# Graph network with layer norm: silu of the last three node groups made by ScalarE alone

## The chip, the cores and the metric

The kernel runs on one core of a Trainium2 chip. The metric is the device time of one execution in microseconds (us); smaller is better. A profile is one further execution, recorded instruction by instruction. In it PE is TensorE, DVE is VectorE, ACT is ScalarE, POOL is GpSimd and SP is the engine that issues most transfers.

## The reference

There are 12,500 nodes with 128 features and 400,000 edges sorted by destination. Each edge carries a message; the messages are summed by destination; each node's sum goes through two small products with silu between them; the result is added to twice the node's own value and normalized.

```python
rbf = jnp.exp(-(distances[:, None] - centers) ** 2 / (2.0 * width * width))
cut = 0.5 * (jnp.cos(jnp.pi * distances / CUTOFF) + 1.0) * (distances <= CUTOFF)
W = (jax.nn.silu(rbf @ fw1 + fb1) @ fw2 + fb2) * cut[:, None]
messages = (h[src] @ pw + pb) * W
agg = jax.ops.segment_sum(messages, dst, num_segments=num_atoms)
h_new = h + (jax.nn.silu(agg @ mw1 + mb1) @ mw2 + mb2)
x = layernorm(x + h_new)        # here h is x
```

The change concerns only the line with `mw1` and `mw2`, and there only how silu is made for the last nodes.

## The kernel before, in words

The order of instructions is written out by hand: every engine executes its own list in the order in which the program issues it, and an instruction waits until what it needs is there.

The work has four stages. First, `project` multiplies all nodes by `pw` and stores the result in memory. Beside it, `pack` drops the edges beyond the cutoff and lays the rest out in 141 steps (`NQ`) of 512 edges. Then the loop over the steps q follows: GpSimd gathers 512 projected source rows with four indirect transfers (L643); TensorE and ScalarE make the edge's filter W (L693, L699, L707, L710); VectorE multiplies filter and gathered rows to messages (`message`, L717) and builds a selection matrix (`place`, L726); TensorE sums the messages by destination (`sum_up`, L742); VectorE adds these sums into `aggT`, the sums of all nodes held on the chip with features as rows (`add`, L765), one or two steps later.

The nodes are finished in 25 groups of four row tiles, 512 nodes each, named by their first row tile t0 = 0, 4, ..., 96; group 96 has 212 nodes. The steps of finishing a group are:

- `node_first` (L772): a bank of PSUM takes the bias and the product with `mw1` (L776, L777). ScalarE writes t = tanh(z/2) to a tile `zt` (L779). The bank is kept.
- `node_silu` (L782): VectorE makes zs = (t + 1) * z from `zt` and the bank (L786). That is twice silu(z). The bank is free then.
- `node_second` (L790): another bank takes bias (L274) and zs times `late["mw2"]` (L277), which is `mw2` halved, so that the factor two goes out again. `rows_times` (L271) issues these products.
- `node_stats` (L795): VectorE adds twice x (L801) and takes the statistics of each row (L805).
- `scales` (L807): for up to four groups together, 18 short VectorE operations on at most 16 columns make the reciprocal root and the shift.
- `normalize` (L836): ScalarE (L844), and at the very end VectorE too (L841), scale the rows; SP issues the store (L137).

As edges are sorted by destination, early nodes are complete before the loop ends. A table `begin` (L888 to L896) says at which step each group starts its four stages, beginning at step 70. Groups whose four stages all come before step 141 are called `early`. Group 88 starts at step 139 but can't end inside the loop: it alone is `last`. It gets `node_first` at step 139 and `node_silu` at step 140, both inside the loop, in `nodes(q)` (L900), which is issued ahead of the step's message. Groups 92 and 96 are in no table. They, and the second half of group 88, are issued by `finish` (L860) behind the loop.

`finish` issues: `node_first` of 92 and 96; then for 88, 92 and 96 in turn `node_second`, `node_stats`, and, after the statistics of one group, `node_silu` of the next group; then `scales` of the three and the normalizations.

There are four banks handed out by `bank()` in the order in which they were given back. Tiles named `zt` share a tag of three buffers with `xT`, tiles named `zs` a tag of three with `hp`.

A branch (L1099) repeats the whole sum in a general way if the layout of the edges broke an assumption; with these inputs it isn't taken. It calls `finish` a second time with all groups.

Of the kernel before, what the change touches and what calls it, by code (L numbers as in the profile page):

```python
# [10 lines left out]
F32 = mybir.dt.float32  # L11
BF16 = mybir.dt.bfloat16
I32 = mybir.dt.int32
AF = mybir.ActivationFunctionType
# [5 lines left out]
P = 128  # L20
# [6 lines left out]
QE = QT * P  # L27
# [30 lines left out]
def kernel(  # L58
# [37 lines left out]
    nc = tc.nc  # L96
# [16 lines left out]
    work = ctx.enter_context(tc.tile_pool(name="work", bufs=2))  # L113
# [4 lines left out]
    def load_x(t0, name="x4", bufs=8):  # L118
        t = work.tile([P, 4, H], F32, name=name, bufs=bufs)
        node_dma(t0, t, x, False)  # L120
        x_sb[t0] = t

    def rows(t0, n=4):
        return [min(P, N - t * P) for t in range(t0, min(t0 + n, NT))]

    def alike(r):


        full = sum(1 for m in r if m == P)
        return [v for v in ((0, full, P), (full, len(r) - full, r[-1])) if v[1]]  # L130
# [65 lines left out]
    for t0 in range(0, 4 * AHEAD_X, 4):  # L196
# [3 lines left out]
    fw2_sb, mw1_sb, mw2_sb = (keep.tile([H, H], F32, name=k)  # L200
                              for k in ("fw2_sb", "mw1_sb", "mw2_sb"))
# [16 lines left out]
    bias_b = {}  # L218
# [52 lines left out]
    def rows_times(to, lT, w, bias_b, r):  # L271

        for a, c, m in alike(r):
            nc.tensor.matmul(to[:m, a:a + c, :], ones_b[:, :m], bias_b[:, :c, :], start=True,  # L274
                             stop=False)
            for k in range(a, a + c):
                nc.tensor.matmul(to[:m, k, :], lT[:, k * P:k * P + m], w, start=False,  # L277
                                 stop=(k == a + c - 1))
# [25 lines left out]
    free = [ps.tile([P, 512], F32, name=f"bank{k}", bufs=1) for k in range(4)]  # L304
    held = []

    def bank():

        while not free:
            go_on(held[0])  # L310
        return free.pop(0)
# [455 lines left out]
    late = {}  # L767


    z_of, zs_of, py_of, st_of = {}, {}, {}, {}  # L770

    def node_first(t0):  # L772

        n = sum(rows(t0))
        pz = bank()
        nc.tensor.matmul(pz[:, :n], bias_b["mb1"][:, 0, :], ones_b[:, :n], start=True, stop=False)  # L776
        nc.tensor.matmul(pz[:, :n], mw1_sb, aggT[:, t0 * P:t0 * P + n], start=False, stop=True)  # L777
        t = work.tile([P, QE], F32, name="zt", tag="xT", bufs=3)
        nc.scalar.activation(t[:, :n], pz[:, :n], AF.Tanh, scale=0.5)  # L779
        z_of[t0] = pz, t  # L780

    def node_silu(t0):  # L782
        n = sum(rows(t0))
        pz, t = z_of.pop(t0)
        s = work.tile([P, QE], F32, name="zs", tag="hp", bufs=3)
        nc.vector.scalar_tensor_tensor(s[:, :n], t[:, :n], 1.0, pz[:, :n], op0=OP.add, op1=OP.mult)  # L786
        free.append(pz)
        zs_of[t0] = s

    def node_second(t0):  # L790

        py_of[t0] = bank()
        rows_times(py_of[t0].rearrange("p (k f) -> p k f", k=4), zs_of.pop(t0), late["mw2"], bias_b["mb2"], rows(t0))

    def node_stats(t0, st):  # L795

        r = rows(t0)
        y, b = x_sb[t0], py_of.pop(t0)
        py = b.rearrange("p (k f) -> p k f", k=4)
        for a, c, m in alike(r):  # L800
            nc.vector.scalar_tensor_tensor(y[:m, a:a + c], y[:m, a:a + c], 2.0, py[:m, a:a + c],  # L801
                                           op0=OP.mult, op1=OP.add)
        free.append(b)
        for k, m in enumerate(r):
            nc.vector.bn_stats(st[:m, k, :], y[:m, k, :])  # L805
# [30 lines left out]
    def normalize(t0, rs, by, both=False):  # L836

        y = x_sb.pop(t0)
        for k, m in enumerate(rows(t0)):
            if both and k:  # L840
                nc.vector.tensor_scalar(y[:m, k, :], y[:m, k, :], rs[:m, k:k + 1], by[:m, k:k + 1],  # L841
                                        op0=OP.mult, op1=OP.add)
            else:
                nc.scalar.activation(y[:m, k, :], y[:m, k, :], AF.Identity, bias=by[:m, k:k + 1],  # L844
                                     scale=rs[:m, k:k + 1])
        node_dma(t0, y, out, True)
# [3 lines left out]
    def scaled(group, st):  # L850

        rs, by = scales(st, sum(len(rows(t)) for t in group))
        ready.extend((t, rs[:, t - group[0]:], by[:, t - group[0]:]) for t in group)

    def statistics():
        st = work.tile([P, 16, 6], F32, name="st")
        nc.vector.memset(st, 0.0)
        return st

    def finish(these, have=()):  # L860

        every = list(have) + these
        for t0 in every[:4]:
            if t0 not in x_sb:
                load_x(t0)
        for k, t0 in enumerate(every):
            if k + 4 < len(every) and every[k + 4] not in x_sb:
                load_x(every[k + 4])
            if k % 4 == 0:
                st = statistics()  # L870
            for t1 in every[len(have) if k == 0 else k + 2:k + 3]:
                if t1 not in have:
                    node_first(t1)
            if k == 0 and not have:
                node_silu(t0)
            node_second(t0)
            node_stats(t0, st[:, k % 4 * 4:])
            if k + 1 < len(every):
                node_silu(every[k + 1])
            if k % 4 == 3 or k + 1 == len(every):  # L880
                scaled(every[k // 4 * 4:k + 1], st)
            if ready and k + 1 < len(every):
                normalize(*ready.pop(0))
        while ready:
            normalize(*ready.pop(0), both=True)
# [10 lines left out]
        at_q += 3 if at_q < NQ - 12 else 2  # L896
    last = [t0 for t0 in begin if begin[t0][3] >= NQ]
    early = [t0 for t0 in begin if t0 not in last]

    def nodes(q):  # L900

        if ready:
            normalize(*ready.pop(0))
        for k, t0 in enumerate(early + last):
            if begin[t0][0] - 5 == q:
                load_x(t0)
            if begin[t0][3] == q and t0 in early:
                if k % 4 == 0:
                    st_of[0] = statistics()
                node_stats(t0, st_of[0][:, k % 4 * 4:])  # L910
                if k % 4 == 3 or k + 1 == len(early):
                    scaled(early[k // 4 * 4:k + 1], st_of[0])
            if begin[t0][2] == q and t0 in early:
                node_second(t0)
            if begin[t0][0] == q:
                node_first(t0)
            if begin[t0][1] == q:
                node_silu(t0)
        if q == NQ - 4:
            for t0 in range(0, NT, 4):  # L920
                if t0 not in begin:
                    load_x(t0)
# [170 lines left out]
    for q in range(added(NQ), NQ):  # L1093
        base_of(q)
        add(q)
    finish([t0 for t0 in tiles if t0 not in begin], last)


    with tc.If(total > 0):  # L1099
# [51 lines left out]
        if E % QE:  # L1151
            again(E - QE, QT - E % QE // P)
        finish(tiles)


# [24 lines left out]
```

## Time and profile before

| what | us |
|---|---|
| median of 3 runs | 816.37 |
| lowest, highest | 815.54, 817.31 |
| time of the profiled execution | 819.14 |
| its span, first to last instruction | 817.3 |
| TensorE busy in the span | 604.2 (74%) |
| VectorE busy | 587.5 (72%) |
| ScalarE busy | 381.1 (47%) |
| GpSimd busy | 569.8 (70%) |
| mean granted clock of TensorE | 0.851 of full |
| L786 on VectorE, 128x512 | 0.67 to 0.68 each |
| L786 on VectorE, 128x212 | 0.36 |
| last gather issued | 784.57 (from the span's start) |
| last addition into `aggT` ends | 792.7 |
| last normalization ends | 810.9 |

The page's busy shares are means over stages of different kind, so they say little about one stage. A row of a chain view gives the start, the length and the instruction (engine, output tile, line) of one link; "issue" is time in which the engine waited for nothing that the profile shows, and a name such as DVEq is the queue of an engine, which loads registers or issues. A row of a group gives busy time, mean duration in ns, and then the idle time of the engine just before such instructions with what ended it. The granted clock is what share of its full clock TensorE was given.

### The profile page before, as it was taken

What the parts mean: (1) busy time and instruction counts of PE and PEld (TensorE: products, weight loads), DVE (VectorE), ACT (ScalarE), POOL (GpSimd) and SP (SyncE); (2) the same over time, 40 slices, a digit from 0 to 9 for tenths busy, and PEclk for the clock granted to TensorE, in tenths of its full rate; (3) what the DMA queues carried; (4) which work ended last, traced back from release to release, by engine and by line L of the source; (5) the groups of instructions that cost most, each with busy time, mean ns of one, the idle gap of its engine ahead of it and who ended that gap; (6) DMA issues with size and microseconds to landing.
All of it is one profiled execution on the core that took longest, in us unless ns stands there. A gap on an engine that the chain in (4) does not pass through costs nothing.

```text
span 817.3 us, 11550 instructions
## 1 busy us (share of the span) xinstructions
PE 604.2 (74%) x3492; PEld 475.7 (58%) x3492; DVE 587.5 (72%) x1785; ACT 381.1 (47%) x536; POOL 569.8 (70%) x585
## 2 busy tenths in 40 slices
PE   6777878768776777866588678887777887688661
PEld 5766657547664555655456556665555665566551
DVE  7962568989978877979796677657566565756764
ACT  6536656434644353253354254636444633454421
POOL 1375477777777777777777777777777777777730
PEclk9978899977987776778779788999889989889875
DMA  6968734342234223332531622723622642371221
GB/s 198 263 201 246 191 85 105 90 117 75 74 107 112 65 65 112 103 78 53 144 87 52 164 65 79 194 68 104 170 79 58 159 122 78 80 188 52 81 83 48
DMA packets 88189, 91.86 MB, mean 112 GB/s; under 512 B 13864, under 2 KB 67832, under 8 KB 88120
## 3 DMA queue, kind: packets, MB, share of 16 engines
q1 hardware_dynamic: 69320, 52.77, 22.6%
q0 software_dynamic: 18544, 38.17, 18.6%
q8 instruction: 29, 0.48, 0.2%
q14 instruction: 40, 0.33, 0.1%
q10 hardware_dynamic: 256, 0.11, 0.1%
HBM read 75.29 MB, written 15.71 MB: 111 GB/s over the span
## 4 chain that ended last, share of the span: by engine, by line
DVE 24%; POOL 20%; DMA 20%; issue 16%; PE 14%; ACT 3%; DVEq 2%; SPq 0%; POOLq 0%; ACTq 0%
POOL quad L643 20%; DMA quad<-proj,srci 18%; DVE hot L726 4%; PE sums L742 4%; PE bank L277 3%; DVE aggT L765 3%; DVE quad L726 2%; PE bank L710 2%; DVE msg L717 2%; DVEq L751 2%; PE ph L693 2%; DVE quad L717 1%; DVE r_d L438 1%; DVE nodes L429 1%; PE bank L595 1%
## 5 line engine op out<-in xcount | busy, mean ns | idle before, releaser
L643 POOL DMA_INDIRECT quad<-proj,srci x532 | 524.9, 987 | 169.6 <-issue 131.7
L710 PEld LDWEIGHTS bank<-fw_sb,s 128*128 128x128 f32 x1128 | 175.2, 222 | 37.1 <-issue 28.8
L710 PE MATMUL bank<-fw_sb,s 128*128 128x128 f32 x1128 | 173.5, 304 | 0.0
L699 ACT ACTIVATE s<-ph 128x1024 f32<-128x1024 f32 (+1 forms) x71 | 72.3, 1018 | 197.9 <-PE ph L693 197.8
L742 PEld LDWEIGHTS sums<-hot,msg 128*128 128x128 f32 x696 | 92.3, 206 | 115.4 <-DVE msg L717 84.8
L742 PE MATMUL sums<-hot,msg 128*128 128x128 f32 x696 | 109.3, 304 | 52.6 <-DVE msg L717 52.5
L742 PE MATMUL sums<-quad,quad 128*128 128x128 f32 x432 | 79.3, 342 | 67.8 <-DVE quad L717 67.6
L742 PEld LDWEIGHTS sums<-quad,quad 128*128 128x128 f32 x432 | 70.2, 247 | 74.3 <-DVE quad L717 74.3
L717 DVE TENSOR_TENSOR msg<-bank,quad 128x512 f32<-128x512 f32 x87 | 59.6, 685 | 71.9 <-DMA quad<-proj,srci 62.7
L726 DVE TENSOR_SCALAR hot<-iota_n,dl,cut 128x128 f32<-128x128 f32 x348 | 98.6, 358 | 12.7 <-PE sums L742 8.9
L693 PE MATMUL ph<-rbf,w_sb 51*128 51x512 f32 x282 | 89.5, 711 | 1.5 <-ACT s L699 1.4
L717 DVE TENSOR_TENSOR quad<-bank,quad 128x512 f32<-128x512 f32 x54 | 37.1, 688 | 56.1 <-DMA quad<-proj,srci 54.3
L765 DVE TENSOR_TENSOR aggT<-aggT,sums 128x128 f32 x212 | 60.4, 285 | 22.3 <-PE sums L742 10.9
L707 PE MATMUL bank<-fb_b,ones_b 96*128 96x512 bf16 x141 | 61.5, 436 | 19.3 <-DVE msg L717 8.7
L683 ACT ACTIVATE rbf<-d,rbf_bias,rbf_scale 128x512 f32<-128x512 f32 (+1 forms) x71 | 57.0, 803 | 37.9 <-DMA d<-near_d 37.7
L726 DVE TENSOR_SCALAR quad<-iota_n,dl,cut 128x128 f32<-128x128 f32 x216 | 61.8, 360 | 3.0 <-issue 0.7
L779 ACT ACTIVATE zt<-bank 128x512 f32<-128x512 f32 (+1 forms) x25 | 14.6, 583 | 81.5 <-PE bank L777 81.5
L844 ACT ACTIVATE x<-x,by,rs 128x128 f32<-128x128 f32 x91 | 37.1, 481 | 30.6 <-DVE by L814 30.6
L277 PEld LDWEIGHTS bank<-pw_sb,xT 128*128 128x128 f32 x260 | 40.0, 222 | 11.3 <-issue 5.1
L684 ACT ACT_TABLE_LOAD x36 | 46.2, 1283 | 0.6
L699 ACT ACT_TABLE_LOAD x36 | 46.2, 1283 | 0.6
L684 ACT ACTIVATE rbf<-rbf 128x512 f32<-128x512 f32 (+1 forms) x71 | 44.7, 630 | 1.5
(169 smaller groups left out, 744.2 us busy)
## 6 DMA issues: line engine op xcount, KB each, us to landing
d<-near_d SPq DMA_DIRECT2D x141, 128.0 KB
x<-in_x_dram SPq DMA_DIRECT2D x48, 256.0 KB
quad<-proj,srci POOLq DMA_INDIRECT x532, 2.6
proj<-hp SPq DMA_DIRECT2D x24, 256.0 KB
out_dram<-x SPq DMA_DIRECT2D x24, 256.0 KB
packed<-zero_i SPq DMA_DIRECT2D x6, 188.0 KB
pair<-packed SPq DMA_DIRECT2D x3, 264.0 KB
r_d<-in_edge_weight_dram SPq DMA_DIRECT2D x3, 256.0 KB
```

Of the source, the lines that this page charges most:

```text
L277: nc.tensor.matmul(to[:m, k, :], lT[:, k * P:k * P + m], w, start=False, stop=(k == a + c - 1))
L643: nc.gpsimd.indirect_dma_start(out=got[:, j, :], out_offset=None, in_=proj if table is None else table, in_offset=bass.IndirectOffsetOnAxi ...
L683: nc.scalar.activation(rbf[:u], d[:u], AF.Square, bias=rbf_bias[:u], scale=rbf_scale[:u])
L684: nc.scalar.activation(rbf[:u], rbf[:u], AF.Exp, scale=-1.0 / (2.0 * width * width))
L693: nc.tensor.matmul(ph[:, h, :], w1_sb[p0:p0 + KR], rbf[p0:p0 + KR], start=True, stop=True)
L699: nc.scalar.activation(s[:, :n], ph[:, :n], AF.Silu)
L707: nc.tensor.matmul(pu, ones_b[:, :P], bias_b["fb2"].rearrange("k j f -> k (j f)"), start=True, stop=False)
L710: nc.tensor.matmul(pu[:, j * H:(j + 1) * H], s[:, j * P:(j + 1) * P], fw2_sb, start=False, stop=(j == QT - 1))
L717: nc.vector.tensor_mul(msg, pu.rearrange("p (j f) -> p j f", j=QT), got_of.pop(q))
L726: nc.vector.tensor_scalar(hot[:, j, :], iota_n[:, :W], dl[:, at[0], at[1]], cut[:, at[0], at[1]], op0=OP.is_equal, op1=OP.mult)
L742: nc.tensor.matmul(pa[:, k * W:(k + 1) * W], msg[:, j, :], hot[:, j, :], start=(j % n == 0), stop=(j % n == n - 1))
L765: nc.vector.tensor_add(to, to, pa[:, k * W:(k + 1) * W])
```

## The change

A set `straight` collects the groups that are finished behind the sums: `last` (88) and what `finish` is given (92 and 96). For these, `node_first` lets ScalarE write silu(z) straight into the tile `zs` and gives the bank back at once; `node_silu` does nothing; `node_second` multiplies by `mw2` itself in place of its half. The early groups keep tanh, the VectorE instruction and the halved weights.

```diff
+    straight = set()
     def node_first(t0):
...
         nc.tensor.matmul(pz[:, :n], mw1_sb, aggT[:, t0 * P:t0 * P + n], start=False, stop=True)
+        if t0 in straight:
+            s = work.tile([P, QE], F32, name="zs", tag="hp", bufs=3)
+            nc.scalar.activation(s[:, :n], pz[:, :n], AF.Silu)
+            free.append(pz)
+            zs_of[t0] = s
+            return
         t = work.tile([P, QE], F32, name="zt", tag="xT", bufs=3)
...
     def node_silu(t0):
+        if t0 in straight:
+            return
...
     def node_second(t0):
         py_of[t0] = bank()
-        rows_times(py_of[t0].rearrange("p (k f) -> p k f", k=4), zs_of.pop(t0), late["mw2"], bias_b["mb2"], rows(t0))
+        rows_times(py_of[t0].rearrange("p (k f) -> p k f", k=4), zs_of.pop(t0),
+                   mw2_sb if t0 in straight else late["mw2"], bias_b["mb2"], rows(t0))
...
     def finish(these, have=()):
         every = list(have) + these
+        straight.update(these)
...
     last = [t0 for t0 in begin if begin[t0][3] >= NQ]
     early = [t0 for t0 in begin if t0 not in last]
+    straight.update(last)
```

In the order of instructions, VectorE loses three entries (L786 of groups 88, 92 and 96), and three entries of ScalarE become silu in the same places. Group 96's first product takes the bank that group 88's silu gave back, in place of another one. The lists of GpSimd and SP are the same up to the branch that isn't taken.

## The prediction

> **What bounds the kernel now.** I read the page first. The profiled execution took 819.14 us, its span is 817.3 us, so 1.84 us lie outside the span. The chain of the whole page is GpSimd's gathers; this change does not touch them. The diff acts on three groups of nodes only (row tiles 88, 92 and 96), and these lie in the last 30 us. So the second view is the chain that ended last, cut to 770 to 818 us (start, us, what):
>
> ```profile
> 788.91 0.38 DVE zs L786
> 789.29 0.01 DVEq L751
> 789.30 0.61 DVE msg L717
> 789.90 0.04 issue
> 789.95 2.09 PE sums L742 x8
> ...
> 797.17 0.70 DVE x L801
> ...
> 798.76 0.60 DVE zs L786
> 799.36 0.04 issue
> 799.40 1.91 PE bank L277 x8
> 801.31 0.02 issue
> 801.33 0.70 DVE x L801
> ...
> 802.93 0.29 DVE zs L786
> 803.21 0.04 issue
> 803.26 0.80 PE bank L277 x2
> ...
> 804.66 0.48 DVE x L801 x2
> ```
>
> In this stretch no engine is full. It is a relay: VectorE makes zs (L786), TensorE multiplies it (L277), VectorE adds and takes statistics (L801, L805), and only then makes the next zs. All three instructions that the change removes (zs for groups 88, 92 and 96) are links of the chain. After 804.66 come statistics, the 18 small operations of `scales`, seven normalizations up to 810.90, the stores and the end.
>
> The third view is the list of groups by form (busy, mean ns, idle before and releaser), for what ScalarE will do instead:
>
> ```profile
> L779 ACT ACTIVATE zt<-bank 128x512 f32<-128x512 f32 x24 | 14.2, 593 | 81.2 <-PE bank L777 81.2
> L699 ACT ACTIVATE s<-ph 128x512 f32<-128x512 f32 x1 | 0.6, 597 | 0.3 <-PE ph L693 0.3
> ```
>
> A tanh of 128x512 from a bank takes 593 ns, the one silu of that size 597 ns. The instruction that replaces tanh costs the same.
>
> The fourth view is TensorE in stretches of 3.41 us (stretch, its length, TensorE busy, granted clock, DMA):
>
> ```profile
> 786.00:789.41 3.41, 2.05 (x8) 0.50 0.32 96
> 789.41:792.83 3.42, 2.61 (x10) 0.50 0.01 2
> 792.83:796.24 3.41, 3.41 (x8) 0.50 0.00 0
> 796.24:799.65 3.41, 1.36 (x11) 1.00 0.26 77
> 799.65:803.07 3.42, 1.75 (x9) 0.50 0.00 0
> ```
>
> The granted clock is half or full for a whole stretch. It rose after the stretch that was fully busy (3.41 of 3.41), not after one busy for 2.61, and fell again after one busy for 1.36. The products of groups 92 and 96 therefore ran at half clock here.
>
> **The change part by part.**
>
> ScalarE: three tanh become three silu, 593 against 597 ns, in the same places of its queue: no cost. All stand behind TensorE's first product (L777). For group 88 ScalarE runs at 781.60, seven us before its zs is wanted. For group 92 it runs 794.83 to 795.43, for group 96 795.80 to 796.15, behind idle times of 7.9 and 0.4 us. Cover: before, zs of 92 was made only at 798.68, so the silu is early by some 3 us against before and by 1.5 us against TensorE, which turns to group 92 at 796.97. Were ScalarE later than that, the gain would shrink one for one.
>
> Does silu need a table? The page lists 36 loads of 1283 ns at L684 (exponential) and 36 at L699 (silu), none at L779: tanh follows silu without one, and in the order of the changed kernel's instructions no load is added. The Trainium skill ("ScalarE: Activation LUTs", section "Table sets: the hidden batching unit") names no set with silu beside tanh and puts a switch at 2.66 us. By the rule the first silu would pay that; it is group 88's, at 781.6, with seven us to spare, and groups 92 and 96 follow with no other set between. By the row nothing, by the rule nothing on the path. I take nothing.
>
> VectorE, group 88: zs runs from 788.61 to 789.29, and the message that the last sums wait for starts at 789.21 right behind it. Its gather is not what it waits for: the last gather was issued at 784.57, and the gathers of this stretch land 2.6 to 3.4 us after issue, so by 788.0. Without zs the message starts at 788.61: **0.60 us** off the path, passed on to the sums (789.95), aggT, both first products and group 88's second product. If the register loads at L751 that stand around it (297 to 714 ns) took its place, it would be 0.2 to 0.3; I take 0.60, since those loads ran beside zs.
>
> Groups 92 and 96, from group 88's addition at 797.17 on. Before, the next addition (group 92) comes at 801.33: addition 0.70 and statistics 0.89 to 798.76, zs 0.60, then 1.97 us in which VectorE waits for the product. Now zs is there at 795.43, and TensorE goes on at 796.97 with bias (0.22 at full clock, as at 772.12 in the chain) and eight passes (0.89 and about 0.16 until the result is seen): ready at 798.24, before VectorE is free at 798.76. So group 92's addition starts at 798.78, not 801.33. Its addition and statistics take 1.60 again, to 800.36, and before them zs of 96 (0.29) and the wait of 1.45 fall away: TensorE needs about 0.7 us at full clock for group 96 and is ready near 799. Its addition starts at 800.38 instead of 804.66: **4.28 us**. Put as removed links: 0.60 + 1.97 + 0.29 + 1.45 = 4.31, the same within the issue gaps. VectorE's own additions and statistics are late next, and then `scales`, whose length is unchanged.
>
> Weights and banks: the second product takes the loaded weights instead of their half (one 128x128 f32 tile either way; the load is some 300 us old): nothing. `mw2_h` stays for the early groups. Group 96 now takes the bank that silu of group 88 gave back at about 782.2, wanted at 794.59: one new wait of TensorE on ScalarE, long over. Behind it stand all second products, so it would cost one for one if ScalarE were 12 us late; it isn't. Queues of SP and GpSimd keep their order; the stores move with the normalizations.
>
> With the clock as in this trace: 0.60 + 4.28 = **4.9 us**.
>
> The clock is the unknown term, and I bound it from both sides. (a) If TensorE stayed at half clock through the second products: group 88's result 0.70 later (0.43 + 1.91 from 795.51), group 92 ready near 800.0 and group 96 added near 801.6, so 3.06 + 0.60 = 3.7 us. (b) With the sums 0.60 earlier, the stretch from 789.41 has about 3.1 busy us in place of 2.61; if that is enough to raise the clock at 792.8, the two first products and group 88's second run at full clock, about half of 3.4 us less: 4.9 + 1.5 = 6.4 us. (c) The times to compare come from other executions. The Trainium skill ("TensorE: Matmul & The Clock Gate", Part 1) says that the 3.4 us window is free-running and doesn't start with the kernel; the rows above agree with the length, and one profile can't show the rest. By the row, before always pays half clock at 92 and 96 and the gain is 4.9; by the rule, in other executions before finds the full clock there, its two waits shrink from 1.97 and 1.45 to about 1.1 and 0.8, and the gain is 0.60 + 0.60 + 1.1 + 0.29 + 0.8 = 3.4. (The same page lets the clock fall only after an idle window; here it fell after 1.36 busy us of 3.41, and I go by the row.) Between 3.4, 4.9 and 6.4 I take **4.4 us**, a little under the trace's own phase, because the trace of before is one of the dearer cases.
>
> **The sum.** The profiled execution would go from 819.14 to about 814.7. On the median of the runs shown: 816.37 - 4.4 = 812.0 us.
>
> **Rivals.**
>
> 1. The clock comes early (case b): gain 6.4, 810.0 us. For: 3.1 of 3.4 busy. Against: 2.61 of 3.42 was not enough, and the phase differs by run. Chance 0.14.
>
> 2. The waits stay: TensorE or ScalarE is late for another reason, and only VectorE's own three pieces go: 0.60 + 0.60 + 0.29 = 1.5 us, 814.9 us, just within what a measurement tells from no change (0.2%, 1.63 us). Against: ScalarE idle for 7.9 us ahead of group 92. The same range holds the case that group 88's zs frees nothing and noise takes more. Chance 0.06. That the change does nothing at all is excluded: the three instructions lie in the chain.
>
> 3. Slower: instruction fetch. The program is shorter by some VectorE instructions in the branch not taken, so later code moves. Place: the jump over that branch (L1099); TensorE's took 3.40 us at 803.3, off the path, the other engines' 0.05 to 0.08. Were two such waits to land on VectorE and SP in the tail, 6.8 - 4.4 = 2.4 us slower, 818.8 us. It decides from 6.0 us on (4.4 + 1.63). Against: the order of instructions up to group 88 is unchanged on every engine, and runs of before spread by only 1.77 us. Chance 0.03.
>
> The likeliest, 4.4 us (3.4 to 4.9 and a run's spread of 0.9 either way), has 0.77: 810.6 to 813.9. With rival 1's and part of rival 2's side the range is 809.8 to 814.2. Faster by over 0.2%: 0.91; within: 0.06; slower: 0.03.
>
> **What would show it.** In the profile after: no zs made by VectorE in the last 30 us; silu near 0.60 us at 781.6 and 794; message right behind aggT, some 0.6 earlier against the last gather; no wait of VectorE for L277 longer than 0.2 us at groups 92 and 96; from group 88's addition to group 96's 3.2 us instead of 7.5. Wrong would be: a table load before a silu in the tail, TensorE waiting on ScalarE for more than a few tenths at L277, or the clock at half through all second products together with a gain over 5 us.

## The result and the profile after

| | before | changed |
|---|---|---|
| median of 8 runs, us | 816.93 (815.54 to 817.99) | 811.14 (808.50 to 814.01) |
| ratio, 95% interval | | 0.9931 (0.9911 to 0.9950) |
| span of the profiled execution | 817.3 | 806.9 |
| start of step 139's sums to the end of the span (the tail) | 31.33 | 24.68 |

The changed kernel is 5.8 us faster, with an interval of 4.1 to 7.3 us. The forecast was 4.4 us and 812.0 us. On some chips a part of the executions, before and after alike, is over 1.5% slower than the fastest; each ratio in this document leaves these out, so it isn't quite the quotient of the medians.

The two spans differ by 10.4 us, far more than the medians. Most of what goes beyond the change lies in front of it: step 139's sums start at 785.97 us before and at 782.22 us after, though until then both kernels have the same instructions in the same order on every engine, but for ScalarE's one for group 88 (0.60 us either way). So single spans say little here: the loop takes a different time in every execution (its play, below). I compare the tail instead, from the first product of step 139's sums (785.97 and 782.22) to the end of the span; it begins behind all the play of the loop and holds every instruction that the change takes away.

This is the chain of waits of the changed kernel in that stretch (start, us, what); from `node_silu` on, line numbers are ten higher than before:

```profile
784.42 0.32 DVEq L751
784.74 0.38 DVE msg L717
785.16 2.09 PE sums L742 x8
...
791.47 0.70 DVE x L811
792.40 0.66 DVE st L815 x3
793.06 0.60 DVE x L811
793.89 0.66 DVE st L815 x3
794.55 0.38 DVE x L811 x2
```

The relay is gone. Between group 88's addition (791.47), group 92's (793.06) and group 96's (794.55) stand only VectorE's own statistics, no zs and no product. (VectorE's additions begin just before the statistics in front of them end, so the chain, which has no overlaps, gives 3.08 us from the first to the last and the timeline 3.00.) The timeline of the same kernel shows what TensorE and ScalarE do meanwhile (start, us, engine, instruction, and in brackets the idle time before it and what ended it):

```profile
789.88 0.83 ACT L781 ACTIVATE zs<-bank 128x512 f32<-128x512 f32 x2 [6.75 <-PE bank L778]
...
791.47 0.69 DVE L811 SCALAR_TENSOR_TENSOR x<-x,bank 128x512 f32<-128x512 f32 x1 [3.48 <-PE bank L277]
791.49 1.05 PE L277 MATMUL bank<-mw_sb,zs 128*128 128x128 f32 x8
...
792.98 0.67 DVE L811 SCALAR_TENSOR_TENSOR x<-x,bank 128x512 f32<-128x512 f32 x1
...
794.47 0.46 DVE L811 SCALAR_TENSOR_TENSOR x<-x,bank 128x128 f32<-128x128 f32 x2
```

The two silu of groups 92 and 96 (merged into one row, 0.83 us, from 789.88 on) stand each behind the first product of its own group. The second product of group 92, the row at 791.49, has no wait ahead of it and takes 1.05 us, where it took 1.89 us before, and VectorE waits for TensorE only once, at group 88.

TensorE's clock after (stretch, length, TensorE busy, granted clock, DMA):

```profile
782.92:786.33 3.41, 2.11 (x10) 0.50 0.26 77
786.33:789.75 3.42, 3.15 (x9) 0.53 0.01 2
789.75:793.16 3.41, 3.41 (x28) 1.00 0.02 5
```

Two stretches run at half clock here and three did before, so the clock is back at full one stretch earlier; the stretch in front of the rise was busy for 3.15 of 3.42 us.

### The profile page after: what moved, and what is told of

It reads as the page before. It is cut to its first block, busy times and chain, and to the rows that moved or that the text cites. A ratio compares the mean times of both kernels' runs of the same rounds, so it can differ in the third digit from the quotient of the medians.

```text
span 806.9 us, 11547 instructions
## 1 busy us (share of the span) xinstructions
PE 598.8 (74%) x3492; PEld 471.6 (58%) x3492; DVE 585.0 (72%) x1782; ACT 381.3 (47%) x536; POOL 567.8 (70%) x585
## 4 chain that ended last, share of the span: by engine, by line
POOL 24%; DVE 21%; issue 20%; DMA 17%; PE 13%; ACT 3%; DVEq 2%; SPq 0%; POOLq 0%; ACTq 0%
POOL quad L643 23%; DMA quad<-proj,srci 13%; PE sums L742 3%; DVE hot L726 3%; PE bank L710 3%; DVE aggT L765 2%; PE ph L693 2%; PE bank L277 2%; DVE quad L726 2%; DVE msg L717 2%; DMA x<-in_x_dram 1%; DVEq L751 1%; DMA pair<-packed 1%; DVE quad L717 1%; DVE st L815 1%
## 5 line engine op out<-in xcount | busy, mean ns | idle before, releaser
L710 PEld LDWEIGHTS bank<-fw_sb,s 128*128 128x128 f32 x1128 | 177.1, 224 | 39.5 <-issue 30.5
L710 PE MATMUL bank<-fw_sb,s 128*128 128x128 f32 x1128 | 175.6, 307 | 0.0
L699 ACT ACTIVATE s<-ph 128x1024 f32<-128x1024 f32 (+1 forms) x71 | 72.3, 1018 | 203.9 <-PE ph L693 203.8
L742 PE MATMUL sums<-quad,quad 128*128 128x128 f32 x432 | 76.7, 334 | 60.8 <-DVE quad L717 60.8
L742 PEld LDWEIGHTS sums<-quad,quad 128*128 128x128 f32 x432 | 67.6, 238 | 68.0 <-DVE quad L717 67.8
L277 PEld LDWEIGHTS bank<-pw_sb,xT 128*128 128x128 f32 x260 | 39.3, 218 | 10.4 <-issue 5.3
L643 POOL DMA_INDIRECT quad<-in_x_dram,srci x32 | 32.9, 1027 | 16.7 <-issue 8.5
```

The lines of the kernel that those rows point to most:

```text
L643: nc.gpsimd.indirect_dma_start(out=got[:, j, :], out_offset=None, in_=proj if table is None else table, in_offset=bass.IndirectOffsetOnAxi ...
L699: nc.scalar.activation(s[:, :n], ph[:, :n], AF.Silu)
L710: nc.tensor.matmul(pu[:, j * H:(j + 1) * H], s[:, j * P:(j + 1) * P], fw2_sb, start=False, stop=(j == QT - 1))
L742: nc.tensor.matmul(pa[:, k * W:(k + 1) * W], msg[:, j, :], hot[:, j, :], start=(j % n == 0), stop=(j % n == n - 1))
```

## The experiments

All parts of a tail are taken from one profile each. "88 to 96" is the time from group 88's addition to group 96's; "clock up" is when the granted clock rises, counted like the tail from the start of step 139's sums. Nothing else in the tail moves: from group 96's addition to the end it is 12.3 to 12.7 us in every kernel of the table.

| kernel | tail | to group 88's addition | 88 to 96 | clock up | time against before on its chip (95%) |
|---|---|---|---|---|---|
| before | 31.33 | 11.20 | 7.49 | 10.3 | |
| changed | 24.68 | 9.25 | 3.00 | 7.3 | 0.9931 (0.9911 to 0.9950) |
| changed, again | 26.11 | 10.65 | 3.00 | 9.7 | 0.9927 (0.9902 to 0.9953) |
| 88 alone | 30.59 | 10.45 | 7.65 | 9.3 | 0.9986 (0.9950 to 1.0023) |
| 92 and 96 alone | 26.45 | 11.00 | 3.00 | 9.8 | 0.9942 (0.9909 to 0.9975) |
| the same, again | 25.56 | 10.01 | 3.00 | 8.8 | 0.9976 (0.9924 to 1.0027) |
| zs earlier, no silu | 26.54 | 11.17 | 3.00 | 10.2 | 0.9988 (0.9951 to 1.0025) |
| the same, again | 24.99 | 9.57 | 3.00 | 7.8 | 0.9929 (0.9894 to 0.9965) |
| VectorE's instruction put back | 27.28 | 10.87 | 3.89 | 10.2 | 0.9958 (0.9940 to 0.9976) |
| all 25 groups | 25.40 | 9.92 | 3.00 | 8.3 | 0.9810 (0.9756 to 0.9864) |
| the same, again | 24.98 | 9.25 | 3.00 | 7.3 | 0.9911 (0.9874 to 0.9948) |
| TensorE kept busy | 24.84 | 9.50 | 3.00 | falls at 5.3, up 8.7 | 0.9885 (0.9831 to 0.9939) |
| the same, loads earlier | 25.89 | 10.31 | 3.01 | falls at 5.7, up 9.1 | 0.9923 (0.9898 to 0.9948) |

A caution on the last column. "88 alone", both runs of "92 and 96 alone", of "zs earlier" and of "all 25 groups", and "TensorE kept busy" ran on two chips on which the kernel before took 1041.8 and 1042.6 us, not 817; their intervals are 3 to 6 us wide either way, as wide as the effect. The kernel before has no profile there; where the same part of the tail can be compared, from group 88's addition on, it has the same length there within 0.2 us. The others ("changed, again", "put back", "the same, loads earlier") ran beside a before of 816.99 us.

**Which of the three links.** One part alone, then the other.

```diff
-        straight.update(these)      # 88 alone
```


> Silu by ScalarE for group 88 alone; groups 92 and 96 keep tanh and the VectorE instruction. Measured also by the tail: from the start of the last gather to the end of the span, 32.7 us before and 26.3 us with the whole change. Theory (each of the three links costs what the chain of before shows): the message starts about 0.6 us earlier, tail 32.1 us, time about 0.6 us below before, which timing can't tell from no change. Rival (the gain is the clock that rises 3.4 us earlier because the sums come sooner): the tail falls to some 30.5 us with group 88 alone, and the time by 1.5 to 2 us.

```diff
-    straight.update(last)           # 92 and 96 alone
```


> Silu by ScalarE for groups 92 and 96; group 88 keeps tanh and its VectorE instruction ahead of the last message. Theory: from group 88's addition to that of group 96 about 3.2 us in place of 7.5, tail 28.0 to 28.9 us, time 3.5 to 4.3 us below before. Rival (clock): with the sums where they were the clock stays as before, and the tail loses less than 3 us.

> Groups 92 and 96 alone again, since on the chip of the first time before took 1041.8 us. Theory: 26.5 us from the start of step 139's sums to the end, as there; time 3.5 to 5 us below before. Rival (upstream play made the gain): tail 29 us or more.

With 88 alone the relay stays as it was. Its chain reads:

```profile
1023.25 0.60 DVE zs L795
1023.85 0.04 issue
1023.90 2.07 PE bank L277 x8
1025.97 0.02 issue
1025.99 0.70 DVE x L811
```

From group 88's addition to group 96's it takes 7.65 us. The last message starts 0.53 us after the addition in front of it, here and with the whole change, in place of 1.12 us: 0.59 us saved. In the kernel before and in the changed one (VectorE; the rows of `aggT` are the additions):

```profile
788.09 0.61 DVE L765 TENSOR_TENSOR aggT<-aggT,sums 128x128 f32 x2 [1.14 <-PE sums L742]
788.61 0.68 DVE L786 SCALAR_TENSOR_TENSOR zs<-zt,bank 128x512 f32<-128x512 f32 x1
789.21 0.68 DVE L717 TENSOR_TENSOR msg<-bank,quad 128x512 f32<-128x512 f32 x1
...
783.89 0.61 DVE L765 TENSOR_TENSOR aggT<-aggT,sums 128x128 f32 x2 [0.71 <-PE sums L742]
784.42 0.68 DVE L717 TENSOR_TENSOR msg<-bank,quad 128x512 f32<-128x512 f32 x1
```

The tail is 0.74 us shorter, not the 2.2 us of the rival (32.7 to 30.5): in this profile the clock didn't rise a whole stretch earlier. (The expectation counts from the last gather; on this chip that lies 10 us ahead of step 139's sums, so I read it on the tail.)

With 92 and 96 alone it takes 3.00 us twice, and the tail is 4.9 and 5.8 us shorter than before. The times don't decide between the two: the interval holds 1 for 88 alone and for one of the two runs of 92 and 96 alone. The tails do: nearly all of the gain belongs to groups 92 and 96.

**Is it the instruction or its place?** No silu at all; VectorE makes zs of both groups, only earlier in its list.

```diff
+            if have and k == 0:
+                for t1 in every[1:]:
+                    node_silu(t1)
             node_second(t0)
             node_stats(t0, st[:, k % 4 * 4:])
-            if k + 1 < len(every):
+            if not have and k + 1 < len(every):
                 node_silu(every[k + 1])
```


> No silu at all: tanh and the VectorE instruction stay for all three groups, but VectorE makes zs of 92 and 96 ahead of group 88's addition, while it waits for TensorE, in place of behind the statistics. Theory (what costs is where zs stands in VectorE's list, not that it is made there): as with 92 and 96 by ScalarE, from group 88's addition to that of group 96 3.2 to 3.4 us, tail 28.0 to 29.0 us, time 3.3 to 4.3 us below before. Rival (the saved VectorE instructions themselves are the gain): no more than a few tenths, tail above 32 us.

> tanh kept, zs of 92 and 96 earlier in VectorE's list, again for its time. Theory: like groups 92 and 96 by silu, 26.5 us of tail, time 3.5 to 5 us below before. Rival (the instruction's own time is the gain): tail above 30.5 us, time within 1 us of before.

VectorE's timeline in the first of the two:

```profile
1026.55 1.09 DVE L795 SCALAR_TENSOR_TENSOR zs<-zt,bank 128x512 f32<-128x512 f32 x2 [2.69 <-ACT zt L786]
1028.23 0.69 DVE L811 SCALAR_TENSOR_TENSOR x<-x,bank 128x512 f32<-128x512 f32 x1 [0.58 <-PE bank L277]
1028.95 0.87 DVE L815 BATCH_NORM_STATS2 st<-x 128x6 f32<-128x128 f32 x4
1029.74 0.67 DVE L811 SCALAR_TENSOR_TENSOR x<-x,bank 128x512 f32<-128x512 f32 x1
```

Both zs fit into VectorE's wait for group 88's product (in the second profile they end just as it is ready), and 88 to 96 is 3.00 us, the same as with silu. VectorE still executes the 0.67 and 0.36 us; they cost nothing where they stand. (Of the two times one is clearly below before, 0.9929, and the other's interval holds 1.) So it was the place behind the statistics that cost 4.5 us, and moving these instructions in the order would have got as much of the tail. The other way round, VectorE's time put back and only that (an addition and product on parts of `aggT` into a tile that nobody reads; no product waits for it):

```diff
+            if have and k + 1 < len(every):
+                n = sum(rows(every[k + 1]))
+                again_t = work.tile([P, QE], F32, name="zt", tag="xT", bufs=3)
+                nc.vector.scalar_tensor_tensor(again_t[:, :n], aggT[:, :n], 1.0,
+                                               aggT[:, QE:QE + n], op0=OP.add, op1=OP.mult)
```


> The whole change, and behind the statistics of groups 88 and 92 VectorE executes one more instruction of the form and size that the change took away, on other data, into a tile that nobody reads. Theory (of the 4.5 us between group 88's and group 96's addition only VectorE's own 0.60 + 0.29 us are busy time, the rest was TensorE standing still for zs): from group 88's addition to group 96's 3.9 us, against 3.0 with the change and 7.5 before; tail 0.9 us above the change. Rival (the form of the instruction, reading and writing between the statistics, costs in itself): 5 us or more.

```profile
800.99 0.69 DVE L811 SCALAR_TENSOR_TENSOR x<-x,bank 128x512 f32<-128x512 f32 x1 [4.66 <-PE bank L277]
...
802.50 0.68 DVE L892 SCALAR_TENSOR_TENSOR zt<-aggT 128x512 f32<-128x512 f32 x1
...
804.88 0.47 DVE L811 SCALAR_TENSOR_TENSOR x<-x,bank 128x128 f32<-128x128 f32 x2
```

It measures 3.89 us: 0.89 us of the 4.49 are VectorE's own, the other 3.6 us were VectorE's wait for TensorE, which had waited for zs. Its time, 813.78 us, is 3.1 us above the changed kernel of the same round (810.67); the tail accounts for 0.9 to 1.2 us of that. In its profile step 139's sums start at 790.12 us against 780.79, so play in front of the tail can account for the rest; that is argued, not shown.

This profile shows one thing more. Its clock rises as late as that of the kernel before (10.2 and 10.3 us):

```profile
796.92:800.33 3.41, 3.41 (x10) 0.50 0.00 0
800.33:803.75 3.42, 2.36 (x21) 1.00 0.28 81
```

Its last sums start 3.38 us after step 139's in place of 3.98, so the 0.60 us of group 88 are won there. But group 88's addition comes after 10.87 us in place of 11.20: only 0.33 us are left. The clock rises where it did, and what starts 0.60 us earlier has 0.60 us more under half clock, in which TensorE does half (its eight sums take 2.09 us in place of 1.05); as an estimate from these two durations 0.30 us should be left. The other late profiles fit: 11.00 and 11.17 us with group 88's zs in place (rises at 9.8 and 10.2), 10.65 without it (9.7).

**Does VectorE's busy time count in the loop?** All 25 groups by silu.

```diff
-    straight.update(last)
+    straight.update(begin)
```


> Silu by ScalarE for all 25 groups, also the 22 that are finished inside the loop: 22 more VectorE instructions of 0.68 us (15 us of busy time) go. Theory (an instruction is worth only what it is on the chain; in the loop the gathers set the step): tail 26.3 us within the clock's play of 1.5, time as with the change, within 1.5 us. Rival (VectorE's busy time counts): up to 15 us faster than the change. A table load more per group would show as time lost on ScalarE, which has room.

> All 25 groups by silu again for its time. Theory, where the gathers set the step of the loop: tail 24 to 25.5 us, time as with the change within 1.5 us (5 to 7 us below before). Rival (VectorE's 15 us in the loop count): 10 us or more below the change.

The tail is as with the change. The time is 1.9 and 0.9% below before, on the two chips where before takes 1042 us. There GpSimd is busy 54 to 56% of the span against 70%, and the gathers have 1 and 3% of the chain that ended last against 20% (before) and 23% (changed) on the other chip. So they don't set the step, and the theory's condition is not met. The changed kernel didn't run there, but groups 92 and 96 alone did: on the first chip all 25 groups are clearly faster than these (0.9810, at most 0.9864, against 0.9942, at least 0.9909), by more than group 88 can give; on the second the intervals overlap. So VectorE's busy time may count there, as the rival says; how much stays open. No table load is added: ScalarE has 76 in all as before, 5 of the 36 at L699 are now at L781. On the chip of 817 us the kernel of the last experiment below has all 25 groups too, and its last gather is issued at 784.59 us, against 780.08, 781.17 and 788.92 in the three others of its round: not earlier, as far as single profiles can tell that lie 9 us apart.

**The clock and what comes next.**

```diff
+    def keep_busy(k):                       # products that nobody reads
+        idle = ps.tile([P, 2, QE], F32, name="ph", bufs=1)
+        for _ in range(k):
+            nc.tensor.matmul(idle[:, 0, :WS], mw1_sb, iota_n, start=True, stop=True)
...
+        if q >= NQ - 2:
+            keep_busy(4 if q == NQ - 2 else 1)
         sum_up(q, msg)
```


> The whole change, and TensorE is kept busy in two waits ahead of the last two sums: five more products of 128x500 into banks that nobody reads (four behind group 88's first product, one behind the sums of step 139); they add nothing to the output. Theory (the tail's rest is partly half clock): no stretch of 3.4 us is idle enough for the clock to fall, so both sums, the first products and group 88's second product run at full clock: from the start of the sums of step 139 to the end 24.7 us with the change (clock up 7.2 us after that start), now about 22.0 to 23.0 us, and time 1.5 to 2.5 us below the change. Rival (the clock doesn't matter since VectorE is the bound, or the added products stand in the way of the sums): within 0.5 us of the change, or later by what an added product overhangs, 0.5 to 1 us.

Both sums run at full clock (1.05 and 1.16 us in place of 2.09), but the last addition to `aggT` comes no earlier behind the last message. VectorE's part of that kernel's chain:

```profile
1011.34 0.29 DVE aggT L770
1011.62 0.04 DVEq L756
1011.66 0.45 issue
1012.11 0.30 DVEq L756
...
1012.68 0.30 DVE aggT L770
```

L756 there is the register load of the place in `aggT` (L751 before). The last addition waits for it: it starts at 1012.68, the sums end at 1011.77. From the start of the last message to the last addition it takes 2.80 us here and 2.85 us with the change, where the sums at half clock end 0.5 us after the last load. TensorE stands idle meanwhile, and the clock falls at 5.3. So the tail, 24.84 us, isn't below the 24.68 of the change's first profile. The next kernel also issues the loads of the last two steps earlier:

```diff
+            if (q, k) in bases:
+                continue
...
+        if q == NQ - 2:
+            base_of(NQ - 2)
+            base_of(NQ - 1)
```


> The whole change, TensorE kept busy as before with five products that nobody reads, and the register loads for the last two additions into aggT issued one step earlier, ahead of the last message. Theory (with TensorE at full clock the register loads at L751 were the next bound: 2.80 us from the last message to the last addition, both with the kept-busy kernel and with the change): from the last message to the last addition 1.9 us, from the start of step 139's sums to group 88's addition about 7 us in place of 9.5 and the end 22 to 22.8 us after that start, against 24.8 and 24.7. Rival (the clock falls all the same): 24 us or more.

The last message to the last addition is 1.94 us, as expected. But the loads now stand ahead of the message:

```profile
784.52 0.29 DVE aggT L772
784.81 0.03 DVEq L758
784.84 0.08 issue
784.92 0.55 DVEq L758
785.47 0.07 issue
785.54 0.31 DVEq L758
785.85 0.07 issue
785.92 0.30 DVEq L758
...
786.48 0.70 DVE msg L722
```

The message starts 2.27 us after the addition in front of it in place of 0.53: 1.7 us lost for 0.9 won. The theory's sum left out that VectorE's queue holds the message behind its loads. The clock falls all the same, at 5.7, as the rival said. Time 810.46 us, as the change.

The last kernel keeps the loads of these two steps there, adds three products that nobody reads ahead of the last step's sums, makes all 25 groups by silu and moves the coefficients of the early groups behind step 139's sums too:

```diff
-    straight.update(last)
+    straight.update(begin)
...
-                    scaled(early[k // 4 * 4:k + 1], st_of[0])
+                    behind.append((early[k // 4 * 4:k + 1], st_of[0]))
+                    if q < NQ - 2:
+                        scaled(*behind.pop())
...
+        if q == NQ - 1:
+            keep_busy(3)
...
+        if behind:
+            scaled(*behind.pop())
+        if q == NQ - 2:
+            base_of(NQ - 2)
+            base_of(NQ - 1)
```


> All 25 groups by silu, register loads of the last two steps earlier, the 18 small operations of the early groups' last scales moved behind step 139's message, and three products that nobody reads between the last two sums to hold the clock. Theory: message 139 no longer waits 5 us for the scales, the last message follows its gather by 2 to 3 us, and then everything as with the earlier register loads: from the last message to the end 20 to 21 us, against 28.1 before and 22.5 with the change; time 2 to 4 us below the change. Rival (VectorE has no room: the scales now stand ahead of the last message): last message no earlier, no gain over the earlier register loads alone.

This one ends worse: last message 5.24 us after the last gather's start, and 23.87 us from there to the end, against 3.82 and 22.48 with the change, as the rival expected. The 18 small operations and then the loads stand between step 139's sums and the last message; VectorE has no hole there. Time 813.49 us (ratio 0.9958, 0.9941 to 0.9975), not better than the change. On this chip no version tried beats the changed kernel.

> The changed kernel once more, beside the last three on one chip. Theory: from the start of step 139's sums to the end 24.5 to 26 us with the clock's play, group 88's to group 96's addition 3.0 us; time 4 to 7 us below before. Rival (the measured 5.8 us were in part the play of what lies upstream of the tail): 2 us or less.

The change once more gave 810.67 us, ratio 0.9927, next to the first measurement. Its clock rose at 9.7 us, half a us before the 10.3 of before: 31.33 - 26.11 = 5.2 us.

## Why the prediction was right

The time lay in the range and the mechanism is the one forecast, but terms of its sum had the wrong size. Step by step:

- ScalarE at no cost: 0.83 us for both silu, no load in the tail, no wait of TensorE on ScalarE for a second product. The table load that the Trainium skill's rule would add ("ScalarE: Activation LUTs"; its 2.66 us stand in the section "What ACT_TABLE_LOAD costs") didn't come: the changed kernel has 76 loads, as before. Right.
- Group 88: 0.60 us forecast at the message, 0.59 us measured there, with 88 alone and with the change alike. The register loads didn't take its place, though they are just behind, as the kept-busy kernel shows. Wrong was to pass 0.60 us on unchanged to group 88's second product "with the clock as in this trace": most of the way lies under half clock that ends at the same point, and 0.33 us arrive.
- Groups 92 and 96: 4.28 us forecast, 7.49 - 3.00 = 4.49 us measured. VectorE's additions overlap the end of the statistics by 0.1 us each, which the sum from the chain left out.
- With the clock as in the trace the forecast was 4.9 us; the same rise of the clock measures 0.33 + 4.49 = 4.8 us. The two errors nearly cancel, which is luck. The earlier clock (case b) occurred in the first profile of the change: 31.33 - 24.68 = 6.65 us, where the forecast was 6.4. The medians of the two measurements, 5.8 and 6.3 us below before, lie between the two; how often each case occurs wasn't measured, and a part of them can be the loop's play.
- The other term that was mis-sized is the step down from 4.9 to 4.4: "in other executions before finds the full clock there". In both profiles with the relay, before and 88 alone, the clock was at full for one stretch only and, but for 0.3 us, back at half when the products of 92 and 96 came (rise at 10.3 and 9.3, fall at 13.7 and 12.7; zs of 92 ready at 13.4 and 12.6). The waits of the relay leave TensorE busy for only 1.36 and 1.35 us of the stretch behind the rise, and behind it the clock falls; with the change the products come in one burst and fit into full clock. That the 3.4 us pattern doesn't begin with the kernel, as the Trainium skill says ("TensorE: Matmul & The Clock Gate", Part 1), agrees with the runs: in two profiles of the changed kernel the rise lies at 789.55 and 790.53 us of the span, 0.98 us apart, which is no multiple of 3.41. What I drew from it for before was wrong as far as these two profiles go; more phases of before weren't profiled.

Rival 2 (the waits stay) is excluded by the 3.00 us, rival 3 (instruction fetch makes it slower) by the ratio of 0.9931 (0.9911 to 0.9950).

## What to carry to other kernels

In a relay between engines the cost of a small instruction is the wait that it causes, not its duration: 0.89 us of VectorE's time stood for 4.5 us. Ask first whether it can move in its engine's list to where that engine waits anyway; that gave the same as taking it away. Ask where the clock rises: work moved forward under half clock towards a fixed rise brought 0.33 us of 0.60. And when a wait is removed, look for what ended just ahead of the old end: here register loads that had no cover left.

## What the runs showed of the hardware that was not expected

- The kernel before took 817 us in the first measurement and beside the last four experiments, and 1041.8 and 1042.6 us on the two chips of the others. On those two TensorE stood still in 17 to 24 stretches of over 4 us ahead of its last product, 116 to 187 us together, against 7 to 11 such stretches and 35 to 51 us in the profiles of the other chips. In one of them it did nothing for 14.9 us from 406.5 us on (92 and 96 alone, first run), until ScalarE's silu of L699, which had stood for 20.77 us itself. What ended that wait the profile doesn't have on this core: it puts 20 to 27% of the chain on these chips to "another core or an unknown queue". What it was is open.
- Kernels with the same instructions up to there start step 139's sums at 780.8 and at 790.1 us on one chip (the change again, and put back). With effects of 5 us the span of a single execution says nothing; a stretch that begins behind the play says more.
- A register load on VectorE's queue takes 0.30 to 0.55 us, and loads in a row hold the arithmetic behind them: three of them put a message off by 1.7 us.
